# A fast matrix product in fp32 on one core: a scheduler's model of transfers, the first sums of the weights, and where a bias is added

## The chip, the core and the metric

The kernel runs on one core of a Trainium2 chip. The core has TensorE (PE, matmuls into PSUM), VectorE (DVE), ScalarE (ACT), GpSimd (POOL) and SyncE (SP, which here only issues DMAs). GpSimd also issues DMAs, among them accumulating ones, which add what they bring to what lies in the target. The metric is the device time in microseconds of one execution; the median of several runs counts.

## What is computed

```python
# x: 1024 x 512, weight: 64 x 512 x 512, lin_w: 512 x 512, lin_b: 512, all float32
out_lin = x @ lin_w.T + lin_b
xv = jnp.einsum('bf,efm->bem', x, weight)
zp = jnp.einsum('bf,efm->bem', jnp.square(x), jnp.square(weight))
interaction = 0.5 * jnp.sum(jnp.square(xv) - zp, axis=1)
return out_lin + interaction
```

The costly part is xv, 64 products of 1024 x 512 by 512 x 512, of which only the sum of squares over the 64 is kept.

## The kernel before

**Groups and trees.** The weights are cut into 16 groups (`NG`). A group holds four quadrants of 1 MB, w11, w12, w21 and w22 (w22 has two buffers, w22a and w22b). Each group's product is made by Strassen's scheme, in Winograd's form, twice over: seven outer products, and each of these again by seven inner ones. One outer product is a `tree(s, g, i)`, in the order `ORDER = (1, 6, 2, 7, 5, 4, 3)`. An inner product (`product`, L481) is two fp32 matmuls of 128x128 by 128x512; the profile shows each such matmul as two records. So a tree has 28 records and a group 196.

**Sums that the scheme needs.** On the side of x there are seven blocks X1 to X7, made once, at the start. Each block has its four parts (copies on ScalarE or sums of 1024 elements a row on VectorE) and inner sums of 256 (`x_sum`), four a block, in seven slots. On the side of the weights, tree 5 takes T1 = w11 + w12 and tree 6 takes T2 = w11 + w12 + w22. `outer_sum` makes these by DMA: it loads w11 into T1 or T2 once more and adds the other quadrants by accumulating DMAs (`load_more`, L422) issued by GpSimd. Later w12 += w22 (before tree 7) and w21 += T2 (before tree 4) are made in the same way. The inner sums `t` of each tree's weights are GpSimd adds of 512.

**From PSUM to the output.** There are four pairs of PSUM banks: b1, b3, b2_0 and b2_1. Within a tree, product 5 goes to b3 and is copied out, product 3 is added there and copied again; product 1 goes to b1 and is copied to a b2 pair, to which products 6, 7 and 4 add. Between these, VectorE takes the sums out (`whole`), and GpSimd finishes some of them. Product 7 can only start when VectorE has taken the b2 pair after product 6 (`outer_sbuf(b2, p53, 1)`). Finished parts are squared on ScalarE and summed over the 64 on VectorE (L297) into acc. For zp the weights are squared on ScalarE (`w_squares`) and summed on VectorE into w2_sum.

**Start.** x and lin_w come in eight and four chunks of 256 KB on SP's and ScalarE's queues, the bias on GpSimd's. Three matmuls of zeros (L326) run first. Then 64 records of x @ lin_w.T (L340) fill all four bank pairs; the last four of them stand behind product 5 of the first tree. VectorE adds the bias on the way out of PSUM (eight adds of 512), and the result, lin, goes to DRAM.

**End.** lin and the sums of 15 groups come back from DRAM (lin into the freed w21 and T1, the sums into T2 and w22a), x comes back and is squared with a factor of -0.5, VectorE adds up (L607), TensorE makes zp's part (L627, 64 records), and VectorE's last adds go to the output.

**The order is planned.** No engine's order is written by hand. `Plan.add` takes each operation with what it costs on an engine, what it reads and writes, and for a DMA how long after its issue it lands (`land`). `Plan.order` first gives each operation a latest time, from TensorE's fixed order (`key`) back through the dependencies; then it plays the kernel forward and lets each engine take the ready operation that is due first. The order found is the order in which instructions are issued; each engine works in that order and waits by semaphores. So a wrong cost in the plan costs no time itself, but it places instructions. SP's DMAs cost 2.4 or 4.8 us of SP's time in the plan, and land 1.5 later; accumulating ones land 8 later. Several DMAs under way don't slow each other in it. `both=True` marks VectorE operations that are planned longer when GpSimd works beside them.

Of the kernel before, what the change touches and what calls it, by code (L numbers as in the profile page):

```python
# [11 lines left out]
F32 = mybir.dt.float32  # L12
# [4 lines left out]
P = 128  # L17
# [9 lines left out]
class Plan:  # L27
# [6 lines left out]


    HOP = 0.3

    def __init__(self):
        self.ops = []
        self.writer = {}  # L40
        self.readers = defaultdict(list)

    def add(self, costs, emit, reads=(), writes=(), key=None, land=0.0, both=False):
        op = SimpleNamespace(
            n=len(self.ops), costs=costs, emit=emit, key=key, land=land,
            deps=set(), succ=[], latest=None, end=None, both=both,
        )
        for r in reads:
            if r in self.writer:
                op.deps.add(self.writer[r])  # L50
        for w in writes:
            op.deps.update(self.readers[w])
            if w in self.writer:
                op.deps.add(self.writer[w])
        for r in reads:
            self.readers[r].append(op.n)
        for w in writes:
            self.writer[w], self.readers[w] = op.n, []
        op.deps.discard(op.n)
        self.ops.append(op)  # L60

    def order(self):
# [11 lines left out]
        while stack:  # L74
            o = stack.pop()
            latest = t if o.latest is None else o.latest
            cost = min(o.costs.values()) + o.land + self.HOP
            for x in o.succ:
                latest = min(latest, ops[x].latest - cost)
            o.latest = latest  # L80
            for d in o.deps:
                waiting[d] -= 1
                if not waiting[d]:
                    stack.append(ops[d])
# [3 lines left out]
        free = dict.fromkeys(pending, 0.0)  # L88
        running = dict.fromkeys(pending)
        times = [self.HOP]  # L90
        done, late, nxt = [], 0.0, 0

        def release(o):
            for e in o.costs:
# [16 lines left out]
        def pick(e, now):  # L111
            if e == PE:
                if nxt < len(chain):
                    o = chain[nxt]
                    if not left[o.n] and ready(o) <= now + 1e-6:
                        return o
                return None
            at = {n: ready(ops[n]) for n in pending[e]}
            for n in sorted((n for n in at if at[n] <= now + 1e-6),
                            key=lambda n: (ops[n].latest, n)):  # L120
                o = ops[n]
                until = now + o.costs[e]
                if not any(
                    now + 1e-6 < at[u] < until - 0.2
                    and ops[u].latest < o.latest
                    and ops[u].latest + late < until + 0.1
                    for u in at
                ):
                    return o
            return None  # L130

        while len(done) < len(ops):
            now = heapq.heappop(times)
            moved = True
            while moved:
                moved = False
                for e in pending:
                    if free[e] > now + 1e-6:
                        continue
                    o = pick(e, now)  # L140
                    if o is None:
                        continue
                    moved = True
                    if e == PE:
                        nxt += 1
                        late = max(late, now - o.latest)
                    cost = o.costs[e]

                    if e == DVE and o.both and free[POOL] > now + 0.1:
                        over = free[POOL] - now  # L150
                        cost += 0.9 * over
                        longer(POOL, 0.35 * over)
                    elif e == POOL and free[DVE] > now + 0.1 and running[DVE].both:
                        over = free[DVE] - now
                        cost += 0.5 * over
                        longer(DVE, 0.9 * over)
                    free[e] = now + cost
                    running[e] = o
                    o.end = free[e] + o.land
                    heapq.heappush(times, free[e])  # L160
                    heapq.heappush(times, o.end + self.HOP)
                    for f in o.costs:
                        pending[f].discard(o.n)
                    done.append((o, e))
                    for x in o.succ:
                        left[x] -= 1
                        if not left[x]:
                            release(ops[x])
# [4 lines left out]
def kernel(  # L173
# [70 lines left out]
        return take  # L244

    half = [P, 2, N]
    for i in range(1, 8):
        make(f"X{i}", [P, 7, Q])
    for q in ("w11", "w12", "w21", "w22a", "w22b", "T1", "T2"):
        make(q, [P, 2, 2, N])  # L250
    for pos in range(4):
# [7 lines left out]
    b2_ring = ring("b2", 2, [P, G, N], ps)  # L259
    acc_ring = ring("acc", 2, [P, NB, MG])  # L260
    w2_sum = sb.tile([P, NK, M], F32, tag="w2_sum", name="w2_sum")
    bias = buf["t4_1"]
    acc_dram = dram.tile([P, NB, M], F32, tag="accd", name="accd")
    lin_dram = dram.tile([P, NB, M], F32, tag="lind", name="lind")

# [34 lines left out]
            reads, writes,  # L300
        )

    def dma(o, i, reads, writes, cost=2.4, land=1.5, queue=nc.sync):
        plan.add({SP: cost}, lambda _: queue.dma_start(o, i), reads, writes, land=land)


    x_src = xT.rearrange("(p k) b -> p k b", k=NK)
# [4 lines left out]
    for k in range(NK):  # L312
        q, r = divmod(k, KH)
        x0, x1, l = f"oa{q}", f"oa{2 + q}", f"ob{q}"
        nc.sync.dma_start(buf[x0][:, r, :], x_src[:, k, ts(0, H)])
        nc.scalar.dma_start(buf[l][:, r, :], lw_src[:, k, :])  # L316
        nc.sync.dma_start(buf[x1][:, r, :], x_src[:, k, ts(1, H)])
        for name in (x0, l, x1):
            landing((name, r), 4.0 + 2.5 * k)
    nc.gpsimd.dma_start(bias, lin_b.partition_broadcast(P))  # L320


    zero = buf["t1_0"]
    nc.vector.memset(zero, 0.0)
    for j in range(3):
        nc.tensor.matmul(  # L326
            buf[("b1", "b3")[j // 2]][:, j % 2, :], zero[:, 0:P], zero, start=True, stop=True
        )
    plan.add({PE: 4.0}, None, (), ("b1", "b3"), key=-2000)

    lin_banks = ["b3", "b1", "b2_0", "b2_1"]
    for k in range(NK):
# [16 lines left out]
                     (bank,), key=PLACE[5] + 0.5 if late else -1000 + 4 * k + g)  # L349
    for g, bank in enumerate(lin_banks):  # L350
        o = ("ob2", "ob3", "c_0", "c_1")[g]
        for j in range(G):
            costs, emit = two_input(DVE, buf[o][:, j, :], buf[bank][:, j, :], bias, False, 512)
            plan.add(costs, emit, (bank, "t4_1"), ((o, j),))
        dma(lin_dram[:, ts(g, G), :], buf[o], ((o, 0), (o, 1)), (o,))

    def block4(i):
        return buf[f"X{i}"][:, 0:4, :].rearrange("p (k q) b -> p k (q b)", k=2)
# [11 lines left out]
    for i, n in ((1, "A11"), (2, "A12"), (4, "A22")):  # L370
        act(block4(i), a_ap(n), None, a_parts(n), (f"X{i}",))

    def x_sum(i, o, a, b, kind, reads, size):

        if kind != "-a - b":
            costs, emit = two_input(DVE, o, a, b, kind == "a - b", size)
        else:
            costs = two_input(DVE, o, a, b, True, size)[0]

            def emit(_):  # L380
                nc.vector.scalar_tensor_tensor(o, a, -1.0, b, ALU.mult, ALU.subtract)

        plan.add(costs, emit, reads, (f"X{i}",), both=True)

    for i, a, b, kind in (
        (5, "A22", "A21", "a - b"),
        (6, "X5", "A11", "-a - b"),
        (7, "A11", "A21", "a - b"),
        (3, "X6", "A12", "-a - b"),
    ):  # L390
        x_sum(i, block4(i), a_ap(a), a_ap(b), kind, a_parts(a, b), 1024)
    for i in ORDER:
        x = buf[f"X{i}"]
        a11, a21, a12, a22 = (x[:, s, :] for s in range(4))
        s1, s2, s4 = (x[:, s, :] for s in range(4, 7))
        for o, a, b, kind in (
            (s1, a21, a22, "a + b"),
            (s2, s1, a11, "a - b"),
            (s4, a12, s2, "a - b"),
            (a21, a11, a21, "a - b"),  # L400
        ):
            x_sum(i, o, a, b, kind, (f"X{i}",), 256)
    for n in a_buf.values():
        plan.add({SP: 0.0}, None, (), (n,) + tuple((n, r) for r in range(KH)))
    for n in ("ob0", "ob1", "ob2", "ob3", "c_0", "c_1"):
        plan.add({SP: 0.0}, None, (), (n, (n, 0), (n, 1)))


# [4 lines left out]

    def load(g, q):
        n = w(g, QUAD[q])
        dma(buf[n], weight[g, q], (), (n,), 4.8)

    def load_more(n, src, reads=()):

        plan.add(  # L420
            {POOL: 1.0},
            lambda _: nc.gpsimd.dma_start(buf[n], src, accum_op=ALU.add),  # L422
            (n,) + reads, (n,), land=8.0,
        )

    def outer_sum(g, which):
        if which < 3:
            n = f"T{which}"
            dma(buf[n], weight[g, 0], (), (n,), 4.8)
            for q in (1, 3)[:which]:  # L430
                load_more(n, weight[g, q])
        elif which == 3:
# [119 lines left out]

    for g in range(NG):
        acc_name[g] = acc_ring()
        load(g, 0)
        outer_sum(g, 2)
        for q in (1, 2, 3):
            load(g, q)
        outer_sum(g, 1)
        w_squares(g, "w12")  # L560
        for idx, i in enumerate(ORDER):
            if i == 1:
# [26 lines left out]
    for g in range(NB // G):  # L589
        n, a = lin_all[g], acc_all[g]  # L590
        dma(buf[a][:, :, 0:edge], acc_dram[:, ts(g, G), 0:edge],
            tuple(("accd", x) for x in range(NG - 1)), (a,))
        dma(buf[n], lin_dram[:, ts(g, G), :], (), (n,))
    for n in xe.values():
        plan.add(
            {DVE: 1.24},
# [80 lines left out]
```

## Time and profile before

| what | value |
|---|---|
| median of three runs | 1419.26 us (1419.24 to 1420.74) |
| the profiled execution's own time | 1420.72 us |
| its span, first to last instruction | 1418.9 us |
| mean granted TensorE clock in the span | 0.999 |
| mean DMA rate | 142 GB/s |
| T<-weight on SP (32, 1 MB each), issue to landing | 4.8 us |
| T<-weight on GpSimd (48, accumulating, 1 MB each) | 8.2 us |
| w<-T on GpSimd (16, accumulating, 1 MB each) | 6.9 us |
| T<-lind and w<-lind on SP (2 each, 512 KB each) | 4.3 and 4.4 us |
| t<-lin_b on GpSimd (the bias, 256 KB) | 6.5 us |

The page counts an instruction's time from its start to its end; matmuls are pipelined, so a matmul's length overlaps the next one's, and the pace is read from start to start. A timeline's row is a run of like instructions on one engine: its start in the span, its length, the engine, the line, what it writes and reads, how many; in brackets, how long the engine had been idle before it and what released it. A row of VectorE at L276 is an add or a subtraction whichever helper made it, so rows are told apart by their tiles.

### The profile page before, as it was taken

The numbers are of one execution on the slowest core, as the hardware profiler recorded it, in microseconds if no ns is written. First come the engines' busy times: TensorE is split into PE (matmuls) and PEld (weight loads), VectorE is DVE, ScalarE is ACT, GpSimd is POOL, SyncE is SP. The second block draws the span as 40 slices with busy tenths as digits, with TensorE's granted clock in tenths as the row PEclk, the third lists the DMA queues.
The fourth block names the chain that finished last, engine by engine and source line by source line (L and its number), as shares of the span: only waits on it lengthen the run. The fifth ranks groups of instructions, "written<-read, shape, count | busy, mean of one in ns | idle before, by whom it ended". The sixth has DMA issues, their size and how long they took to land.

```text
span 1418.9 us, 10383 instructions
## 1 busy us (share of the span) xinstructions
PE 1408.6 (99%) x3270; PEld 621.9 (44%) x3270; DVE 1082.0 (76%) x957; ACT 681.8 (48%) x692; POOL 1014.1 (71%) x693
## 2 busy tenths in 40 slices
PE   9999999999999999999999999999999999999998
PEld 4444444444444444444444444444444444444443
DVE  4779596876958678596877959687795867869685
ACT  2346363554635446373544636355463644537331
POOL 3587786867769686786958678586777868678660
PEclk9999999999999999999999999999999999999999
DMA  9666372655737275472746637265573727546331
GB/s 327 184 162 167 95 179 74 189 123 148 176 88 162 86 182 148 118 178 73 182 108 168 162 100 182 74 182 122 148 181 90 162 79 191 139 123 144 102 106 60
DMA packets 47286, 200.96 MB, mean 142 GB/s; under 512 B 19008, under 2 KB 20032, under 8 KB 24704
## 3 DMA queue, kind: packets, MB, share of 16 engines
q0 software_dynamic: 11600, 84.15, 31.4%
q1 hardware_dynamic: 35056, 115.09, 22.7%
q10 hardware_dynamic: 576, 1.05, 0.2%
q8 instruction: 27, 0.44, 0.1%
q14 instruction: 27, 0.22, 0.0%
HBM read 177.34 MB, written 6.16 MB: 129 GB/s over the span
## 4 chain that ended last, share of the span: by engine, by line
PE 95%; DMA 2%; DVE 2%; POOL 1%; issue 0%; ACT 0%; ACTq 0%; DVEq 0%; SPq 0%
PE b L481 93%; PE b L627 2%; DMA w<-weight 1%; DVE X L276 1%; DMA ob<-lin_wT 1%; POOL ob L276 0%; POOL c L276 0%; DVE w_sum L297 0%; DVE c L276 0%; DVE ob L276 0%; POOL oa L276 0%; ACT oa L290 0%; ACTq L316 0%; POOL t L276 0%; DVE p L276 0%
## 5 line engine op out<-in xcount | busy, mean ns | idle before, releaser
L481 PE MATMUL b<-t,X 128*128 128x512 f32 x1792 | 808.2, 593 | 4.0 <-DVE oa L276 2.6
L481 PEld LDWEIGHTS b<-t,X 128*128 128x128 f32 x1792 | 340.4, 190 | 434.8 <-issue 429.0
L481 PE MATMUL b<-w,X 128*128 128x512 f32 x768 | 358.1, 592 | 0.0
L276 POOL TENSOR_TENSOR t<-w 128x512 f32<-128x512 f32 x128 | 171.2, 1337 | 147.6 <-PE b L481 91.8
L288 ACT COPY p<-b 128x1024 f32<-128x1024 f32 x160 | 161.1, 1007 | 170.6 <-PE b L481 170.6
L481 PEld LDWEIGHTS b<-w,X 128*128 128x128 f32 x768 | 145.9, 190 | 183.7 <-issue 183.4
L276 POOL TENSOR_TENSOR t<-w,t 128x512 f32<-128x512 f32 x128 | 167.7, 1310 | 57.7 <-PE b L481 57.7
L290 ACT ACTIVATE oa<-oa 128x1024 f32<-128x1024 f32 x128 | 133.7, 1057 | 148.0 <-DVE oa L276 146.1
L297 DVE TENSOR_REDUCE acc<-oa 128x16 f32<-128x1024 f32 x128 | 153.7, 1212 | 39.2 <-ACT oa L290 39.2
L481 PE MATMUL b<-T,X 128*128 128x512 f32 x384 | 180.5, 592 | 0.0
L288 ACT COPY b<-b 128x1024 f32<-128x1024 f32 x112 | 111.8, 999 | 141.0 <-PE b L481 140.5
L297 DVE TENSOR_REDUCE w_sum<-wsq 128x16 f32<-128x1024 f32 x128 | 152.2, 1209 | 9.2 <-ACT wsq L290 9.2
L290 ACT ACTIVATE c<-c 128x1024 f32<-128x1024 f32 x64 | 67.6, 1057 | 160.2 <-DVE c L276 93.7
L276 DVE TENSOR_TENSOR oa<-b,p 128x1024 f32<-128x1024 f32 x96 | 116.9, 1218 | 34.5 <-PE b L481 34.5
L276 POOL TENSOR_TENSOR t<-T 128x512 f32<-128x512 f32 x64 | 85.3, 1333 | 65.7 <-issue 35.4
L481 PEld LDWEIGHTS b<-T,X 128*128 128x128 f32 x384 | 73.1, 190 | 92.4 <-issue 84.9
L276 DVE TENSOR_TENSOR p<-b,p 128x1024 f32<-128x1024 f32 x80 | 97.7, 1221 | 20.8 <-PE b L481 19.1
L276 DVE TENSOR_TENSOR ob<-b,p 128x1024 f32<-128x1024 f32 x48 | 58.6, 1221 | 70.2 <-PE b L481 70.2
L290 ACT ACTIVATE wsq<-w 128x1024 f32<-128x1024 f32 x96 | 98.2, 1057 | 15.1 <-DMA w<-weight 13.3
L276 POOL TENSOR_TENSOR t<-T,t 128x512 f32<-128x512 f32 x64 | 86.4, 1350 | 18.1 <-PE b L481 18.1
L276 DVE TENSOR_TENSOR p<-b,oa 128x1024 f32<-128x1024 f32 x32 | 39.2, 1224 | 65.6 <-PE b L481 65.6
L276 DVE TENSOR_TENSOR oa<-b,oa 128x1024 f32<-128x1024 f32 x64 | 78.3, 1223 | 9.8 <-PE b L481 9.7
(55 smaller groups left out, 1338.7 us busy)
## 6 DMA issues: line engine op xcount, KB each, us to landing
w<-weight SPq DMA_DIRECT2D x48, 1024.0 KB, 4.9
T<-weight POOLq DMA_DIRECT2D x48, 1024.0 KB, 8.2
T<-weight SPq DMA_DIRECT2D x32, 1024.0 KB, 4.8
w<-weight POOLq DMA_DIRECT2D x16, 1024.0 KB, 8.2
w<-T POOLq DMA_DIRECT2D x16, 1024.0 KB, 6.9
w22a<-weight SPq DMA_DIRECT2D x8, 1024.0 KB, 11.1
w22b<-weight SPq DMA_DIRECT2D x8, 1024.0 KB, 11.3
oa<-xT SPq DMA_DIRECT2D x8, 256.0 KB, 6.4
```

The lines of the kernel that those rows point to most:

```text
L276: f(o, a, b)
L288: nc.scalar.copy(o, i)
L290: nc.scalar.activation(o, i, func)
L297: lambda _: nc.vector.tensor_reduce(o, i.rearrange("p a (m e) -> p a m e", e=E), axis=AX.X, op=ALU.add),
L481: nc.tensor.matmul(buf[b][:, j, :], buf[f"X{i}"][:, SLOT[p], ts(j, P)], op, start=first, stop=True, skip_group_check=True,)
L627: nc.tensor.matmul(buf[bank][:, j, :], buf[xe[h, k // KH]][:, k % KH, ts((g * G + j) % (NB // 2), P)], w2_sum[:, k, :], start=(k == 0), st ...
```

## The change

The diff has five parts.

1. The plan's model of transfers. A DMA now costs SP 0.45 us, GpSimd 0.9, and has a time on the wire (`move`) which all DMAs share, one after the other (`wire`), and then lands. SP may issue a DMA only when it is due within 50 us (`AHEAD`). The landings of the first chunks are set a little later.
2. T1 and T2 of group 0 are made by VectorE from the loaded quadrants, two adds of 1024 each, and not by DMA. The loads of each group stand ahead of its sums in the program.
3. The inner sums of x are made for X1 alone (four operations of 256) and then for X2 to X7 together (four of 1536), in one tile that holds all seven.
4. lin leaves PSUM by four ScalarE copies of 1024 and goes to DRAM without the bias. At the end each of the four target buffers is filled with the bias by two broadcast DMAs on SP, and lin is added by an accumulating DMA.
5. Two matmuls of zeros run at the start instead of three.

```diff
+    AHEAD = 50.0
...
-            cost = min(o.costs.values()) + o.land + self.HOP
+            cost = min(o.costs.values()) + o.move + o.land + self.HOP
...
+                if e == SP and o.latest - self.AHEAD > now + 1e-6:
+                    heapq.heappush(times, o.latest - self.AHEAD)
+                    return None
...
+                    if o.move:
+                        wire = max(wire, free[e]) + o.move
+                        o.end = wire + o.land
...
+    x_all = sb.tile([P, 7, 7, Q], F32, tag="x_all", name="x_all")
     for i in range(1, 8):
-        make(f"X{i}", [P, 7, Q])
+        buf[f"X{i}"] = x_all[:, i - 1]
...
-    def dma(o, i, reads, writes, cost=2.4, land=1.5, queue=nc.sync):
-        plan.add({SP: cost}, lambda _: queue.dma_start(o, i), reads, writes, land=land)
+    def dma(o, i, reads, writes, move=1.75):
+        plan.add({SP: 0.45}, lambda _: nc.sync.dma_start(o, i), reads, writes, land=2.0, move=move)
...
-            landing((name, r), 4.0 + 2.5 * k)
-    nc.gpsimd.dma_start(bias, lin_b.partition_broadcast(P))
+            landing((name, r), 4.3 + 2.6 * k)
...
-    for j in range(3):
+    for j in range(2):
         nc.tensor.matmul(
-            buf[("b1", "b3")[j // 2]][:, j % 2, :], zero[:, 0:P], zero, start=True, stop=True
+            buf["b1"][:, j, :], zero[:, 0:P], zero, start=True, stop=True
         )
...
         o = ("ob2", "ob3", "c_0", "c_1")[g]
-        for j in range(G):
-            costs, emit = two_input(DVE, buf[o][:, j, :], buf[bank][:, j, :], bias, False, 512)
-            plan.add(costs, emit, (bank, "t4_1"), ((o, j),))
-        dma(lin_dram[:, ts(g, G), :], buf[o], ((o, 0), (o, 1)), (o,))
+        act(buf[o], buf[bank], None, (bank,), (o,))
+        dma(lin_dram[:, ts(g, G), :], buf[o], (o,), (("lind", g),))
...
-    for i in ORDER:
-        x = buf[f"X{i}"]
-        a11, a21, a12, a22 = (x[:, s, :] for s in range(4))
-        s1, s2, s4 = (x[:, s, :] for s in range(4, 7))
+    for lo, hi in ((0, 1), (1, 7)):
+        a11, a21, a12, a22, s1, s2, s4 = (x_all[:, lo:hi, s, :] for s in range(7))
+        names = tuple(f"X{i + 1}" for i in range(lo, hi))
         for o, a, b, kind in (
             (s1, a21, a22, "a + b"),
             (s2, s1, a11, "a - b"),
             (s4, a12, s2, "a - b"),
             (a21, a11, a21, "a - b"),
         ):
-            x_sum(i, o, a, b, kind, (f"X{i}",), 256)
+            x_sum(names, o, a, b, kind, names, Q * (hi - lo))
...
-        dma(buf[n], weight[g, q], (), (n,), 4.8)
+        dma(buf[n], weight[g, q], (), (n,), 3.5)
...
-            {POOL: 1.0},
+            {POOL: 0.9},
             lambda _: nc.gpsimd.dma_start(buf[n], src, accum_op=ALU.add),
-            (n,) + reads, (n,), land=8.0,
+            (n,) + reads, (n,), land=2.5, move=5.5,
         )
 
     def outer_sum(g, which):
-        if which < 3:
+        if g == 0 and which < 3:
+            o, a, b = (("T1", "w11", "w12"), ("T2", "w22a", "T1"))[which - 1]
+            for c in range(NCB):
+                costs, emit = two_input(DVE, buf[o][:, c], buf[a][:, c], buf[b][:, c], False)
+                plan.add(costs, emit, (a, b), (o,), both=True)
+        elif which < 3:
             n = f"T{which}"
-            dma(buf[n], weight[g, 0], (), (n,), 4.8)
+            dma(buf[n], weight[g, 0], (), (n,), 3.5)
...
-        load(g, 0)
-        outer_sum(g, 2)
-        for q in (1, 2, 3):
+        for q in range(4):
             load(g, q)
         outer_sum(g, 1)
+        outer_sum(g, 2)
...
-        dma(buf[n], lin_dram[:, ts(g, G), :], (), (n,))
+        for j in range(G):
+            dma(buf[n][:, j, :], lin_b.partition_broadcast(P), (), (n,), 1.0)
+        load_more(n, lin_dram[:, ts(g, G), :], (("lind", g),))
```

## The prediction

> **What bounds the kernel now.** I read the page's busy row first, then TensorE's timeline from end to end, then the timeline of the engine that ends each of its gaps.
>
> ```profile
> PE 1408.6 (99%) x3270; PEld 621.9 (44%) x3270; DVE 1082.0 (76%) x957; ACT 681.8 (48%) x692; POOL 1014.1 (71%) x693
> ...
> PEclk9999999999999999999999999999999999999999
> DMA  9666372655737275472746637265573727546331
> ```
>
> TensorE has work almost all the time and no other engine is near full, so only time at which TensorE doesn't advance can be won. Its pace without a wait is read from any long row, such as 66.60 to 71.75 for 12 records: 0.429 us a record, and two records make one fp32 matmul. 3270 records at 0.429 are 1403 us of a span of 1418.9. The other 16 us are start, gaps and end; the timeline of TensorE shows all of them.
>
> ```profile
> 1.46 4.64 PE L326 MATMUL b<-t 128*128 128x512 f32 x6 [1.46 <-DVE t L324]
> 5.93 25.91 PE L340 MATMUL b<-ob,oa 128*128 128x512 f32 x60
> 33.01 1.96 PE L481 MATMUL b<-t,X 128*128 128x512 f32 x4 [1.16 <-DVE ob L276]
> 34.80 1.88 PE L340 MATMUL b<-ob,oa 128*128 128x512 f32 x4
> ...
> 45.10 1.88 PE L481 MATMUL b<-T,X 128*128 128x512 f32 x4
> 49.35 3.68 PE L481 MATMUL b<-t,X 128*128 128x512 f32 x4 [2.37 <-DVE oa L276]
> 52.83 1.91 PE L481 MATMUL b<-T,X 128*128 128x512 f32 x4
> ...
> 1371.27 1.88 PE L481 MATMUL b<-w22b,X 128*128 128x512 f32 x4
> 1373.15 1.95 PE L481 MATMUL b<-t,X 128*128 128x512 f32 x4
> 1375.32 1.98 PE L481 MATMUL b<-w22b,X 128*128 128x512 f32 x4 [0.22 <-DVE oa L276]
> 1377.58 1.98 PE L481 MATMUL b<-t,X 128*128 128x512 f32 x4 [0.27 <-DVE oa L276]
> 1379.71 1.96 PE L481 MATMUL b<-t,X 128*128 128x512 f32 x4
> ```
>
> Columns: start, length, then the work. Four records should take 1.72 us from start to start. **Gap A**: 60 records from 5.93 should hand over at 31.68; the next start is 33.01, and its four take 1.79, so 1.40 is lost. **Gap B**: four from 45.10 should hand over at 46.82, the next start is 49.35 (2.53 lost), and the four after it take 3.48, half speed, with the next four 0.03 late: 1.79 more. Together 4.32. **Gap C**: the steps at the end are 1.88, 2.17, 2.26, 2.13 and 1.80 instead of 1.72: 1.66 lost. Between 55 and 1371 no start is late. The zero matmuls at the start take 4.47 us (1.46 to 5.93).
>
> Who is late in A and B is VectorE:
>
> ```profile
> 18.04 1.42 DVE L276 TENSOR_TENSOR X<-X 128x256 f32<-128x256 f32 x4
> 28.65 1.22 DVE L297 TENSOR_REDUCE w_sum<-wsq 128x16 f32<-128x1024 f32 x1 [9.19 <-ACT wsq L290]
> ...
> 31.58 1.28 DVE L276 TENSOR_TENSOR ob<-b,t 128x512 f32<-128x512 f32 x2
> ...
> 39.29 8.87 DVE L276 TENSOR_TENSOR X<-X 128x256 f32<-128x256 f32 x8
> 48.08 1.21 DVE L276 TENSOR_TENSOR oa<-b,p 128x1024 f32<-128x1024 f32 x1
> ```
>
> VectorE stands idle 9.19 us with X sums ready, because next in its written order is a reduction whose square waits for w12 until 27.57. So the bias adds that empty b3 start at 31.58, though its last matmul ended near 5.93 + 52 x 0.429 + 0.2 = 28.4 (A), and eight X sums run from 39.29 at 1.10 us each, not 0.34, because GpSimd adds run beside them; the add that product 7 needs waits behind them (B). The order was written with four loads due earlier than they came.
>
> **Part by part, against the profiled execution (1420.72 us).**
>
> Third zero matmul removed. In the timeline of weight loads, each beside the record before its own, the zeros' stand at 1.46 (two), 2.48, 3.33, 4.18 and 5.04 and lin's first at 5.51; so records two to six start at 2.48 to 5.51, and lin at 5.93. With four zero records lin takes the fifth's place, 5.04, if its data is there. Its two chunks land about 4.7: SP's fifth issue, at 4.67, was released by the first lin_w chunk, and the first x chunk was no later. **Gain 0.90, bounds 0.5 and 0.9.** A rule speaks against it: the Trainium skill (TensorE: Matmul & The Clock Gate, "Why this matters for your kernels") wants 4 us of matmuls to warm the clock, and 4 x 0.85 are 3.4. In this trace the pace turns from 0.85 to 0.43 between 5.04 and 5.51, 3.6 to 4.0 us after the first. By the rule, lin begins cold, which costs nothing against zeros: cold lin still advances, cold zeros don't. A cold stretch longer by one 3.4 us window (the page, "What's actually happening") would cost 3.4/2 = 1.7 and make this part -0.8. The row stands nearer, as lin follows without a hole: I keep 0.9.
>
> Bias leaves the start. Out: 8 VectorE adds (1.28 per pair, 5.1 us) and the 256 KB broadcast on POOL's queue. In: 4 ScalarE copies from PSUM, about 1.0 each by the row of the p copies (1.01). ScalarE was busy 10.3 us of 32 to 54, so four more fit. b3 has its 52nd record's end near 5.04 + 52 x 0.429 + 0.2 = 27.5 after the shift, the copy is done by 29 if ScalarE isn't held, and the first product wants b3 at 5.04 + 60 x 0.429 = 30.8. What can hold it is a square queued ahead that waits for a load. **A: gain 1.2 of 1.40**, bounds 0 and 1.4.
>
> Wide sums of x. Before, 28 sums of 256, 16.4 us busy. After, 4 of 256 and 4 of 1536. From paces, start to start, 256 take 0.335 and 1024 take 1.14, so 1536 take about 1.68 (estimate from these two rows): 1.3 + 6.7 = 8.0. They can't start until all seven X blocks are there: the last x chunk lands near 12.9 (ScalarE's wait for it ends 12.27, VectorE's last block from x is at 13.96), and three blocks of 1.14 after it end near 16.5, so the wide sums end near 23 with nothing in between.
>
> T1 and T2 of group 0. Out: 2 loads and 3 accumulating DMAs of 1 MB, and 3 POOL triggers of 0.86. In: 4 VectorE adds of 1024, 1.14 each: 4.6 us. Inputs: T2's load had landed by 15.64 and w11 by 18.00, about 2.4 us per MB with nothing beside them; so in order w11, w12, w22a, w21 land near 15.6, 18, 20.4 and 22.8. Before, w12 took until 27.5. VectorE from 13: 3.4 of blocks, 6.7 wide, 4.6 for T, 2.3 of w12's reductions: T2 is ready near 30. Beside POOL's four t adds of w11 (18.00 to 24.4 before) the two engines hold each other up; the worst row, 1.10 for 0.34, adds at most POOL's own 6.4 us. So between 27.7 (reductions later) and 36.4. Product 5 of the second tree, the first user, is due at 37.65 (30.8 + 4 products x 1.72), and POOL needs one t add of 1.3 to 1.9 before it. Met in the middle by over 5 us, short by 0.6 at the worst end.
>
> With these VectorE has no X sums left after 39, and the add before product 7 starts when its bank is ready. **B: gain 4.2 of 4.32**; bounds 0 (another late operation takes the place) and 4.32. The half-speed stretch goes with the gap: after an idle of 2.37 four records took 3.48, after the 1.16 of A 1.79, and the granted clock of 32 to 54 is 0.92. The same page and section put the fall after about 3.4 us of idling; by that B's 2.5 would stay warm and its removal would be worth 2.5 only. The row decides: 4.3.
>
> The model of transfers only writes another order; no instruction gets longer. What it moves: SP no longer issues more than 50 us ahead of a due time. w22b went out at 36.32 for a first use at 193.63; that moves to a stretch where the DMA share is 0.55. T2's chain (load at 82.79, first product straight from T2 at 133.55) is held only until 133.6 - 25 (its three links by the planner's new costs) - 50 = 59, before its buffer is free. The waits at 55 to 1371 cost TensorE nothing now, so nothing is to be won there: **0**, bounds 0 and a loss of 3 (15 groups at 0.2).
>
> Bias at the end. Out: 4 loads of 512 KB on SP. In: 8 bias broadcasts of 256 KB on SP (issue 0.35 to 0.45 each) and 4 accumulating DMAs on POOL (0.86 each), each waiting for its two broadcasts. Behind a waiting trigger on POOL stand the t adds of the last tree (1371.79, 1373.02) and the oa add at 1374.26. Bounds: a 1 MB accumulate took 8.2 us, so 512 KB less; the broadcast at the start took 6.5 in full traffic, the 256 KB stores at the end 2.2. The w21 pair, free at 1371.6, would be complete near 1371.6 + 2 + 4 + 7 = 1385 instead of 1376. Its adds on VectorE ran at 1377.45 and 1385.18; moved later they leave VectorE to the trees in gap C, and they are not needed before 1398.27, when the first output add ran. POOL's 3.4 us of triggers and their waits work the other way. **C: gain 0.4**, bounds +1.6 and -4. The end from 1390 is 56 records of TensorE and one output add; nothing of it changes.
>
> Sum: 0.9 + 1.2 + 4.2 + 0 + 0.4 = 6.7. From the profiled 1420.72 that is 1414.0. The three runs were 1419.24, 1419.26 and 1420.74, so the profiled one stands at their upper end; from the median it would be 1412.6. The half-speed stretch of B, 1.8 us, may be what sets it apart, and then 1414.0 counts. I reckon from the middle of the two, 1420.0: **1413.3**.
>
> **Rivals.**
> 1. The head keeps a gap (12%): T2, or the square in front of a bank copy, is late, TensorE waits 2 to 3 us near 37 and the clock halves again for 3.4 us. For it: the tight worst end above. Against: w12 comes some 9 us earlier. A loss of 4.3 leaves 6.7 - 4.3 = 2.4: 1417.6.
> 2. Slower by POOL's waiting triggers at the end (10%): four accumulations each hold POOL until a broadcast has landed. If it stands 3 us at each of four, 12 us, the last trees' t adds come late; TensorE loses about 10 and a half-speed stretch of 1.8: 6.3 - 11.8 is 5.5 slower, 1425.5. It decides from about 9 us of standing. For it: an in-order queue and waits that weren't there. Against: T1's pair comes 12 us before w21's, and the planner counts 3.5 us for a broadcast.
> 3. No new order without a price (6%): one wait of 0.4 us in each of 15 groups eats 6: 1419.3. Against: no late start in 1300 us now.
>
> **Numbers.** The forecast's case has 72%, with its own range 1410.8 to 1416.4. Apart by over 0.2% (2.8 us, about what a measurement can tell here): faster below 1416.4, slower above 1422.1. Of rival 1 a third is still faster (a shorter wait) and the rest between, as is rival 3; of rival 2 a fifth ends between. Faster 0.76, same 0.16, slower 0.08. The range goes from all gaps closed (1419.26 - 0.9 - 1.4 - 4.3 - 1.7 = 1411.0, rounded down) to rival 1's 1417.6.
>
> **What would show it.** Lin starts at 5.0; the first product at 30.8 with no gap from VectorE; four records at 1.72 throughout 30 to 60 and a clock that stays full; T2's adds done by 36; w12's squares begin before 21, not 27.6; VectorE's X sums 8 instead of 28, all before 30; no late start in the groups. Wrong would be a gap near 37 ended by POOL's t, one ended by ScalarE's copy of a lin bank, or, near 1360 to 1385, POOL idle on a DMA.

## The result and the profile after

| | before | after |
|---|---|---|
| median (runs) | 1420.0 us (8; 1418.01 to 1421.02) | 1414.91 us (8; 1414.23 to 1415.85) |
| ratio, 95% interval | | 0.9965, 0.9954 to 0.9976 |
| profiled span | 1418.9 us | 1413.5 us |
| start of the last matmul record | 1413.69 us | 1408.08 us |

The change is 0.35% faster, 5.1 us of medians, and 5.61 us at TensorE's last record. The page's busy row and its chain by engine, of the changed kernel:

```profile
PE 1405.5 (99%) x3268; PEld 621.4 (44%) x3268; DVE 1079.4 (76%) x933; ACT 680.6 (48%) x696; POOL 1012.5 (72%) x693
...
PE 99%; DVE 1%; issue 0%; DVEq 0%
```

No engine's busy time moved by more than 3.1 us, and TensorE still sets the end: between its first matmul and its last the chain holds one stretch of another engine. So the gain must lie in TensorE's gaps and in its pace. Its timeline (start, length, work, then in brackets what ended an idle stretch):

```profile
1.46 3.78 PE L333 MATMUL b<-t 128*128 128x512 f32 x4 [1.46 <-DVE t L331]
5.04 26.64 PE L347 MATMUL b<-ob,oa 128*128 128x512 f32 x60
31.52 1.88 PE L490 MATMUL b<-t,x_all 128*128 128x512 f32 x4
33.23 1.88 PE L347 MATMUL b<-ob,oa 128*128 128x512 f32 x4
...
45.25 1.88 PE L490 MATMUL b<-t,x_all 128*128 128x512 f32 x4
46.97 1.88 PE L490 MATMUL b<-T,x_all 128*128 128x512 f32 x4
...
1334.46 1.88 PE L490 MATMUL b<-t,x_all 128*128 128x512 f32 x4
1338.05 3.67 PE L490 MATMUL b<-t,x_all 128*128 128x512 f32 x8 [1.71 <-DVE oa L284]
...
1369.03 1.88 PE L490 MATMUL b<-t,x_all 128*128 128x512 f32 x4
1370.74 1.88 PE L490 MATMUL b<-w22b,x_all 128*128 128x512 f32 x4
1372.46 3.60 PE L490 MATMUL b<-t,x_all 128*128 128x512 f32 x8
```

Gaps A (31.7) and B (47) are gone: from 31.52 on, each four records take 1.72. Gap C after 1360 is gone too: the steps from 1369.03 are 1.71 and 1.72. But the 60 lin records take 26.48 from 5.04 to 31.52, not 25.75, since the clock is still at half speed for the first of them. And there is a **new gap D**: four records from 1334.46 should hand over at 1336.18, and the next starts at 1338.05.

**Accounts.** The trace's record of the granted clock gives the time at which it rises: 5.11 before, 6.50 after. Until then a record takes 0.85 us, after it 0.43, so a rise that comes 1 us later costs 0.5. With that, the start of the last record in every profile of this study is

last record = 1401.17 + 0.86 x (zero matmuls) + rise / 2 + what TensorE lost by waiting.

Here 0.86 is a zero matmul's two records at the full clock. The constant was set by one run (the bias at the start, below). A second run without any late start (squares on ScalarE, below), with its rise 1.8 us earlier, gives the same constant within 0.01. For the pair: A 1.40, B 4.32, C 1.66 and one zero 0.86 come in; the later rise takes 0.70 and D 1.95. Sum 5.59 of 5.61.

ScalarE's squares of w12 and then VectorE after, in the timelines of the start:

```profile
17.42 2.00 ACT L298 ACTIVATE wsq<-w 128x1024 f32<-128x1024 f32 x2 [4.03 <-DMA w<-weight]
```

```profile
17.49 1.73 DVE L284 TENSOR_TENSOR T<-w,w 128x1024 f32<-128x1024 f32 x1 [1.71 <-DMA w<-weight]
19.14 2.82 DVE L284 TENSOR_TENSOR x_all<-x_all 128x1536 f32<-128x1536 f32 x1
21.89 2.28 DVE L284 TENSOR_TENSOR T<-w,w 128x1024 f32<-128x1024 f32 x1
24.09 1.75 DVE L284 TENSOR_TENSOR x_all<-x_all 128x1536 f32<-128x1536 f32 x1
...
28.56 1.21 DVE L284 TENSOR_TENSOR T<-w22a,T 128x1024 f32<-128x1024 f32 x1
29.70 1.75 DVE L284 TENSOR_TENSOR x_all<-x_all 128x1536 f32<-128x1536 f32 x1
31.37 2.33 DVE L305 TENSOR_REDUCE w_sum<-wsq 128x16 f32<-128x1024 f32 x2
```

The 9.19 us of idling before is gone: w12 is there at 17.4, ten microseconds earlier. T2 is done at 29.8 and the last sum of x at 31.4, where before X sums ran until 51. The question is which of the five parts did this.

### The profile page after: what moved, and what is told of

It is laid out like the page before. It is cut to its first block, busy times and chain, and to the rows that moved or that the text cites. A ratio compares the mean times of both kernels' runs of the same rounds, so it can differ in the third digit from the quotient of the medians.

```text
span 1413.5 us, 10316 instructions
## 1 busy us (share of the span) xinstructions
PE 1405.5 (99%) x3268; PEld 621.4 (44%) x3268; DVE 1079.4 (76%) x933; ACT 680.6 (48%) x696; POOL 1012.5 (72%) x693
## 4 chain that ended last, share of the span: by engine, by line
PE 99%; DVE 1%; issue 0%; DVEq 0%
PE b L490 95%; PE b L347 2%; PE b L637 2%; DVE w L607 0%; PE b L333 0%; DVE oa L284 0%; DVE acc L305 0%; DVE w22a L284 0%; DVEq L683 0%; DVE t L331 0%
## 5 line engine op out<-in xcount | busy, mean ns | idle before, releaser
L490 PE MATMUL b<-t,x_all 128*128 128x512 f32 x1792 | 806.1, 592 | 1.7 <-DVE oa L284 1.7
L490 PEld LDWEIGHTS b<-t,x_all 128*128 128x128 f32 x1792 | 340.3, 190 | 430.7 <-issue 423.6
L490 PE MATMUL b<-w,x_all 128*128 128x512 f32 x768 | 358.1, 592 | 0.0
L490 PEld LDWEIGHTS b<-w,x_all 128*128 128x128 f32 x768 | 145.9, 190 | 183.7 <-issue 172.7
L284 POOL TENSOR_TENSOR t<-w,t 128x512 f32<-128x512 f32 x128 | 174.1, 1360 | 66.7 <-PE b L490 66.5
L490 PE MATMUL b<-T,x_all 128*128 128x512 f32 x384 | 180.4, 592 | 0.0
L284 POOL TENSOR_TENSOR t<-T 128x512 f32<-128x512 f32 x64 | 91.7, 1433 | 58.1 <-issue 33.1
L490 PEld LDWEIGHTS b<-T,x_all 128*128 128x128 f32 x384 | 73.0, 190 | 91.8 <-issue 91.8
L284 POOL TENSOR_TENSOR c<-oa,p 128x1024 f32<-128x1024 f32 x32 | 89.3, 2791 | 0.1
L284 POOL TENSOR_TENSOR ob<-ob,p 128x1024 f32<-128x1024 f32 x32 | 89.3, 2789 | 0.0
```

The source lines that it names most:

```text
L284: f(o, a, b)
L490: nc.tensor.matmul(buf[b][:, j, :], buf[f"X{i}"][:, SLOT[p], ts(j, P)], op, start=first, stop=True, skip_group_check=True,)
```

## The experiments

Each run's loss by waiting comes from the formula above, and its place from the timeline. "New" and "old" are the planner's transfer model; part 2 is T1 and T2 on VectorE, 3 the wide sums, 4 the bias at the end. The expectations set theories against each other. For gaps A and B: M blames the order planned with too early landings, T the transfers at the start, V VectorE's own work, and W the work and the traffic together. For gap D, D1 blames a square beside GpSimd's operations. For the zeros, Z1 ties the clock's rise to TensorE's first work, Z2 does not.

| run | model, parts, zeros | median us | rise | lost by waiting, us |
|---|---|---|---|---|
| before | old, none, 3 | 1420.0 | 5.11 | A 1.40, B 4.32, C 1.66 |
| after | new, 2 3 4, 2 | 1414.91 | 6.50 | D 1.95 |
| model alone | new, none, 3 | 1433.84 | 6.86 | 16.3 near 39, 3.2 in C |
| without the model | old, 2 3 4, 2 | 1413.45 | 6.85 | 0.88 after 1370 |
| squares marked | new, 2 3 4, 2 | 1413.55 | 6.98 | D 0.81 |
| three zeros | new, 2 3 4, 3 | 1415.13 | 4.43 | D 1.94 |
| T alone | old, 2, 3 | 1415.81 | 6.12 | A 0.27, C 1.68 |
| T by DMA | new, 3 4, 2 | 1430.85 | 6.82 | 17.6 near 38 |
| narrow sums | new, 2 4, 2 | 1415.09 | 6.12 | D 1.94 |
| bias at the start | new, 2 3, 2 | 1413.64 | 7.03 | none |
| squares on ScalarE | new, 2 3 4, 2 | 1412.95 | 5.24 | none |
| one zero | new, 2 3, 1 | 1414.79 | 7.87 | 0.74 for data near 4 |
| bias at the start, old model | old, 2 3, 2 | 1420.54 | 5.82 | A 5.9, C 1.7 |

### The transfer model alone

The kernel before with part 1:

```diff
+                if e == SP and o.latest - self.AHEAD > now + 1e-6:
...
+                    if o.move:
+                        wire = max(wire, free[e]) + o.move
...
-        dma(buf[n], weight[g, q], (), (n,), 4.8)
+        dma(buf[n], weight[g, q], (), (n,), 3.5)
```

> The kernel before with part 1 of the change alone: the planner's new transfer model (wire, SP's issue 50 us ahead at most, later landings). Every instruction stays, only orders move. Theory M (the order was planned with loads due too early, and that alone opened gaps A and B): VectorE no longer stands idle about 9 us behind the square of w12, gaps A (1.4 us) and B (4.3 us) close, span near 1413 to 1414. Theory W (the gaps close because work and traffic leave the start: bias adds, T1 and T2 by DMA, small sums of x): at least half of A and B stays, span 1416 or more, first products after 33 us or a half-speed stretch between 35 and 60 us.

Ratio 1.0089 (1.0074 to 1.0104): slower by 13 us. Theory M falls. GpSimd's timeline in this run:

```profile
30.22 0.88 POOL L430 DMA_DIRECT2D w<-weight  x1 [2.98 <-ACT wsq L298]
30.81 1.18 POOL L430 DMA_DIRECT2D T<-weight  x1
34.52 1.27 POOL L284 TENSOR_TENSOR t<-w 128x512 f32<-128x512 f32 x1 [2.54 <-PE b L489]
35.75 0.84 POOL L430 DMA_DIRECT2D T<-weight  x1
51.86 1.25 POOL L284 TENSOR_TENSOR t<-T 128x512 f32<-128x512 f32 x1 [15.26 <-DMA T<-weight]
```

T2's second addition is the third trigger, behind w12's and T1's and behind a t add that waits for TensorE; in the kernel before it was the first of the three, at 28.21. It goes out at 35.75 and lands 16 us later beside the other accumulations, while TensorE stands 13.6 us and then runs at half speed. Under the new model the planner put this chain last; which item of part 1 does that (the shared wire, the new costs or the limit on SP) no run separates. Gap A, meanwhile, is gone in this run: VectorE's bias adds for b3 start at 30.14, not behind an X sum.

### T1 and T2 by VectorE alone

The kernel before with part 2, old planner:

```diff
+        if g == 0 and which < 3:
+            o, a, b = (("T1", "w11", "w12"), ("T2", "w22a", "T1"))[which - 1]
+            for c in range(NCB):
+                costs, emit = two_input(DVE, buf[o][:, c], buf[a][:, c], buf[b][:, c], False)
+                plan.add(costs, emit, (a, b), (o,), both=True)
...
```

> The kernel before with part 2 alone: T1 and T2 of group 0 are four VectorE adds, loads in front of sums. Old transfer model, old small sums, bias at the start, three zeros. Theory T (the start's transfers made the gaps: five of nine MB leave, so w12 lands near 18 us instead of 27.5 and nothing holds VectorE): gaps A and B both close, first product near 31.7, no late start from then to 60 us; span 1412.5 to 1414. Theory V (VectorE's own work made them, 16.4 us of small sums and 5.1 of bias adds, to which 4.6 come): A or B stays with 1.4 us or more, span 1415 or more.

Theory T holds: ratio 0.9972 (0.9961 to 0.9983), A shrinks to 0.27, B is gone. TensorE's timeline:

```profile
6.44 25.91 PE L340 MATMUL b<-ob,oa 128*128 128x512 f32 x60
32.38 1.95 PE L486 MATMUL b<-t,X 128*128 128x512 f32 x4
34.17 1.88 PE L340 MATMUL b<-ob,oa 128*128 128x512 f32 x4
...
46.19 1.88 PE L486 MATMUL b<-t,X 128*128 128x512 f32 x4
```

Here VectorE still has 28 small sums and eight bias adds, and small sums run as late as 49. Six of them run ahead of the bias adds for b3, from 28.95 to 30.96, and A's 0.27 is likely theirs; no other start before 60 us is late. VectorE still idles once, 5.93 us, but only until w12 lands at 18.1 (its square runs at 18.06), so its work after that is in time. The span, 1414.1, lies 0.1 above what was expected: the clock rose late (6.12) and C stays, at 1.68.

### The changed kernel without part 2

```diff
-        if g == 0 and which < 3:
+        if False:
```

> The changed kernel with part 2 taken back: T1 and T2 of group 0 by loads and accumulating DMAs, all else as changed. Theory T: TensorE waits for T2 near 38 us as in the run with the transfer model alone, 10 us or more, span 1423 or more. Theory V: with small sums and bias adds gone VectorE is free, gap under 2 us before 60 us, span under 1416.

Ratio 1.0084 (1.0067 to 1.0100). By its timeline TensorE waits 15.35 us for a t add on T2, then runs at half speed:

```profile
35.11 3.60 PE L490 MATMUL b<-w,x_all 128*128 128x512 f32 x8
54.05 5.65 PE L490 MATMUL b<-t,x_all 128*128 128x512 f32 x8 [15.35 <-POOL t L284]
```

So part 2 is not only enough for most of the gain; without it the rest of the change loses 10 us. The edit leaves the group's loads ahead of its sums in the program, and still w12's squares begin only at 27.40: that order in the program alone does not bring w12 sooner.

### The changed kernel without the model, and without model and part 4

The first run puts back the old costs and landings and takes out the wire and the limit on SP:

```diff
-    AHEAD = 50.0
...
-        plan.add({SP: 0.45}, lambda _: nc.sync.dma_start(o, i), reads, writes, land=2.0, move=move)
+        plan.add({SP: cost}, lambda _: queue.dma_start(o, i), reads, writes, land=land)
```

> The changed kernel with the old transfer model put back, parts 2 to 5 kept. Theory M: VectorE or ScalarE again waits for a load in front of ready work, a gap of 2 us or more before 60 us, span 1415.5 or more. Theory W: no gap before 60 us, as w12 lands near 17.5 us without the T traffic in front of it; span within 1 us of 1413.5, apart from what the end does.

No gap before 60 us, as theory W has it, and T. It has 0.88 of late starts after 1370 and no D, and its runs (1413.29 to 1414.09) lie below all of the changed kernel's. Beside these parts the model wins nothing. The second run takes part 4 back too, so that VectorE adds the bias at the start:

> The changed kernel with the bias back at the start and the old transfer model: parts 2, 3 and 5 alone. Theory T (part 2 closes the gaps, the model is not needed for it): no late start before 60 us beyond 0.3. The model's worth is then only what the end shows: if the new model places the end better, the late starts of the kernel before come back after 1360, 1.2 to 1.7 us in sum, span 1413 to 1414.5; if not, 1412.2 as with the new model.

(Its edit is the one above together with that of the next section.) The forecast for the start failed. All of the gain is gone (ratio 1.0002, 0.9993 to 1.0011), by a gap A of 4 us with a half-speed stretch behind it; C is back as well. TensorE's timeline:

```profile
5.04 26.31 PE L341 MATMUL b<-ob,oa 128*128 128x512 f32 x60
35.31 2.54 PE L486 MATMUL b<-t,x_all 128*128 128x512 f32 x4 [3.96 <-DVE ob L276]
37.63 3.04 PE L341 MATMUL b<-ob,oa 128*128 128x512 f32 x4
```

In the changed kernel, ScalarE's timeline has the copy of the first lin bank as soon as it is full:

```profile
28.28 1.01 ACT L296 COPY ob<-b 128x1024 f32<-128x1024 f32 x1 [8.86 <-PE b L347]
```

In the run without model and part 4 the same work stands on VectorE, behind T2 and a wide sum; its timeline:

```profile
31.08 1.21 DVE L276 TENSOR_TENSOR T<-w22a,T 128x1024 f32<-128x1024 f32 x1
32.22 1.74 DVE L276 TENSOR_TENSOR x_all<-x_all 128x1536 f32<-128x1536 f32 x1
33.89 2.47 DVE L276 TENSOR_TENSOR ob<-b,t 128x512 f32<-128x512 f32 x4
```

The bank is full near 28, as there, and is emptied from 33.89. With small sums (T alone) the same planner let the bias adds in at 30.96.

### The changed kernel with the bias at the start, and with narrow sums

```diff
-        act(buf[o], buf[bank], None, (bank,), (o,))
+        for j in range(G):
+            costs, emit = two_input(DVE, buf[o][:, j, :], buf[bank][:, j, :], bias, False, 512)
+            plan.add(costs, emit, (bank, "t4_1"), ((o, j),))
...
```

> The changed kernel with part 4 taken back: eight bias adds on VectorE at the start, the bias broadcast on GpSimd's queue, plain loads of lin at the end. Theory T: no gap before 60 us, as w12 still lands early. Theory V: gap A of 1 us or more at 31.5. At the end both expect what the old end gave or less: late starts of 0.2 to 0.5 us each after 1360, 1.7 in sum at most; the gap of 1.95 us at 1336 stays if it comes from a square beside GpSimd's adds, and goes if the bias DMAs or their waits made it.

No late start anywhere, D included, and its runs (1413.23 to 1414.06) lie below all of the changed kernel's. By its expectation, D's going would speak for the bias DMAs; the section on gap D shows why it does not. The new planner, asked for the same VectorE adds, puts the first two between T2's first half and a wide sum (VectorE's timeline):

```profile
26.88 1.21 DVE L284 TENSOR_TENSOR T<-w22a,T 128x1024 f32<-128x1024 f32 x1
28.55 1.29 DVE L284 TENSOR_TENSOR ob<-b,t 128x512 f32<-128x512 f32 x2 [0.46 <-PE b L349]
29.75 1.75 DVE L284 TENSOR_TENSOR x_all<-x_all 128x1536 f32<-128x1536 f32 x1
```

So the model does have a worth beside parts 2 and 3: with the bias on VectorE it is 7.6 us (A 5.9 and C 1.7 against nothing). At the start, part 4 and the model each cover for the other, and the change has both. The sums of x were undone by one line:

```diff
-    for lo, hi in ((0, 1), (1, 7)):
+    for lo, hi in ((0, 1), (5, 6), (1, 2), (6, 7), (4, 5), (3, 4), (2, 3)):
```

> The changed kernel with part 3 taken back in its work: 28 sums of 256 instead of 4 and 4 of 1536. Theory T: VectorE's sums take more time, but nobody waits: no gap before 60 us, span within 0.8 of 1413.5 (the clock's rise at the start moves it by that much). Theory V: a gap of 1 us or more in front of product 7 of the first tree, near 45 us.

As theory T has it: the loss is D's 1.94, the same as with wide sums (1.95). With the new planner and ScalarE's copies, part 3 is worth nothing.

### Gap D: the square behind GpSimd

The changed kernel's timelines of GpSimd and of VectorE at the gap:

```profile
1330.06 0.88 POOL L426 DMA_DIRECT2D w<-T  x1 [0.94 <-PE b L490]
1330.66 2.66 POOL L284 TENSOR_TENSOR oa<-p,oa 128x1024 f32<-128x1024 f32 x1
1332.99 1.56 POOL L284 TENSOR_TENSOR t<-T 128x512 f32<-128x512 f32 x1
1336.48 1.27 POOL L284 TENSOR_TENSOR t<-w22b 128x512 f32<-128x512 f32 x1 [1.93 <-issue]
```

```profile
1330.66 4.99 DVE L607 SCALAR_TENSOR_TENSOR w<-w 128x1024 f32<-128x1024 f32 x1
1335.57 1.21 DVE L305 TENSOR_REDUCE acc<-oa 128x16 f32<-128x1024 f32 x1
1336.70 1.21 DVE L284 TENSOR_TENSOR oa<-b,p 128x1024 f32<-128x1024 f32 x1
```

A square (1.26 us at 1322.07 in the same kernel) starts with GpSimd's add and ends 1.1 us after the second of GpSimd's two operations (1334.55), so it seems to have stood through both. Behind it stand a reduction and then the sum that product 7 waits for. Two runs tried it. The first only tells the planner that GpSimd holds the squares up:

```diff
-            (n,), (n,),
+            (n,), (n,), both=True,
```

> The changed kernel; the four squares of x at the end are marked as operations that GpSimd's adds hold up, so that the planner keeps them apart. Theory D1 (the new gap of 1.95 us at 1336 is a square of 1.26 us that ran 4.99 us beside two GpSimd operations, with the sum for product 7 queued behind it): no square over 2.5 us, no gap at 1336, span 1411.3 to 1411.8. Theory D2 (the gap comes from another cause, such as the DMAs that GpSimd issues there): the sum for product 7 is late again, span 1413 or more.

Neither expectation was met: the square is placed as before and takes 4.98, but the reduction behind it moved, so D falls to 0.81. The second takes the squares off VectorE:

```diff
-            {DVE: 1.24},
-            lambda _, x=buf[n]: nc.vector.scalar_tensor_tensor(
-                x, x, -0.5, x, ALU.mult, ALU.mult
-            ),
+            {ACT: 1.07},
+            lambda _, x=buf[n]: nc.scalar.activation(x, x, AF.Square, scale=0.5 ** 0.5),
...
```

(The last add, not shown here, then subtracts where it added.)

> The changed kernel with the four squares of x at the end on ScalarE (square of x times the root of one half) and subtracted in the last add instead of added; nothing of the result is left out. Theory D1 (a square of VectorE that starts beside a run of GpSimd operations waits until GpSimd pauses, and the gap at 1336 is that wait): the sums behind it run on time, no late start at 1336, the last matmul 1.9 us earlier for the same rise of the clock, span 1411.2 to 1412.4. Theory D2 (another operation or the DMAs there make it): a late start of 1 us or more between 1325 and 1345.

D is gone, as D1 says, with the bias DMAs still in place, and TensorE doesn't start late once after its first product. The span, 1410.9, lies below the 1411.2 to 1412.4 that were expected, as the clock rose early (5.24). TensorE's timeline at the place:

```profile
1332.12 1.88 PE L490 MATMUL b<-w,x_all 128*128 128x512 f32 x4
1333.84 5.31 PE L490 MATMUL b<-t,x_all 128*128 128x512 f32 x12
1338.98 1.88 PE L490 MATMUL b<-w,x_all 128*128 128x512 f32 x4
```

It is the best version: median 1412.95 (1412.34 to 1413.71), ratio to before 0.9948 (0.9933 to 0.9964). The interval overlaps that of the change, but its four runs all lie below the changed kernel's eight. In the run with the bias at the start, the same square begins a hundredth before GpSimd's t add, and there it is GpSimd that waits (VectorE's timeline, then GpSimd's):

```profile
1328.10 1.21 DVE L609 SCALAR_TENSOR_TENSOR w<-w 128x1024 f32<-128x1024 f32 x1
```

```profile
1328.11 2.34 POOL L284 TENSOR_TENSOR t<-T,t 128x512 f32<-128x512 f32 x1 [0.38 <-PE b L494]
```

The square takes its own 1.21, the t add 2.34 for 1.27. So D went there because the order is another, and not because the bias DMAs did. What decides which engine goes on is not shown: in the changed kernel, too, the square's start is marked first, by 0.004 us, and there it was the square that waited.

### The zero matmuls

```diff
-    for j in range(2):
+    for j in range(3):
...
```

> The changed kernel with the third matmul of zeros put back, in b1. Theory Z1 (the clock rises a fixed time after TensorE's first work, and two zero matmuls are too few to cover it): lin starts at 5.93, the clock rises near 5.1 as in the kernel before, the first product starts at 31.7 against 31.5, 0.2 us slower. Theory Z2 (the rise falls at a time that doesn't depend on the number of zeros and differs from run to run by up to 1.7 us or so): the rise lies anywhere from 5 to 8 us, and the third zero costs 0.43 to 0.9 us for a given rise.

The second run has one, on top of the bias at the start:

```diff
-    for j in range(2):
+    for j in range(1):
```

> The changed kernel with the bias back at the start (no late start after the first product in its run) and one matmul of zeros instead of two. Theory Z2 (the clock's rise keeps its own time; a zero matmul costs 0.86 us at full pace where data could have run): lin starts at about 4.75, when its first chunks land, against 5.04; the rise anywhere from 4.4 to 8.5; 0 to 0.3 us faster than with two for the same rise. Theory Z1 (the rise needs unbroken work from the start, so the pause from 3.3 to 4.75 puts it off): the rise at 8.2 us or later, 0.5 us or more slower.

With three, the clock rose at 4.43, the earliest of all and before the 5 to 8 that Z2 gave, which by the formula won back the third zero's 0.86 in that execution. Over the profiles, the rise lies at 4.43, 5.11, 6.12 and 6.86 with three zeros and at 5.24, 5.82, 6.12, 6.50, 6.82, 6.85, 6.98 and 7.03 with two, so Z1's fixed time falls. The trace agrees with the Trainium skill (TensorE: Matmul & The Clock Gate, "What's actually happening"), which has the clock judged in free-running windows of 3413 ns: in the kernel before the stretches between two changes of the clock are 44.37 and 3.41 us, 13 windows and one. Where a window boundary falls is chance, so one profile can't price a zero matmul. With one zero, TensorE stands from 3.5 to 4.65 until data lands, as its timeline has it:

```profile
1.46 2.07 PE L335 MATMUL b<-t 128*128 128x512 f32 x2 [1.46 <-DVE t L333]
4.65 27.60 PE L349 MATMUL b<-ob,oa 128*128 128x512 f32 x60 [1.11 <-DMA ob<-lin_wT]
```

It loses 0.74 by that and wins 0.86, next to nothing for the same rise; but the rise came at 7.87, and its five runs (1414.23 to 1415.81) lie above the four with two zeros (1413.23 to 1414.06). In the profiled execution the pause did put the rise off. A window of this run ended at 4.45 (7.87 less 3.41), nearly where the run with three zeros had its rise (4.43); there the clock rose, here only a window later, 1.7 us of work. Counted from the starts of its records, TensorE had stood 1.7 us in that window here and 0.6 there. How often this happens, and whether three zeros bring the rise forward on average, stays open, with one trace of each.

## The prediction against the runs

**The total** was right: 1413.3 with 1410.8 to 1417.6, against 1414.91; 6.7 us were forecast from the middle of the runs, 5.1 came. That it came so near is in part luck: C won 1.26 more than forecast, for a reason that stays open, and D, which was not foreseen, took 1.95.

**A and B** were right in size: 1.2 and 4.2 forecast, 1.40 and 4.32 came, the half-speed stretch of B with them. The steps of the transfers' part held: w11, w12 and w22a in time, w12's squares at 17.42 (before 21 was asked), T2 ready at 29.8 (27.7 to 36.4), a sum of 1536 at a pace of 1.67 (1.68). Two signs came late: the first product at 31.52 (30.8), as the clock rose late, and the end of the last X sum at 31.4 (before 30), for which no matmul waited.

**Whose gain it is** was in part wrong. The forecast gave A to the bias adds that leave VectorE and B to T1, T2 and the wide sums together, because no X sums would be left after 39. The runs show the traffic: taking two loads and three accumulations of group 0 away closes both gaps to 0.27 under the old planner, with the bias adds in place and small X sums until 49, while the new planner without this loses 13 us. The wide sums are worth nothing. Moving the bias adds off VectorE, given 1.2, is worth nothing at the start under the new planner and 5.9 us under the old one with wide sums; the parts are not terms of a sum.

**The third zero** was given 0.9, with bounds of 0.5 and 0.9. The place was right (lin at 5.04), and 0.86 is its price for a given rise. The step that failed is the bound: the clock rose 1.4 us later, which the rule's reading in the text allowed for (-0.8 for one more window) and the range of this term left out. It came to 0.16.

**C** was given 0.4, for bias adds that come later and leave VectorE to the trees. C went altogether, +1.66, and the runs don't give it to one part. Under the old planner it is 1.66, 1.68 and 1.7 with the old end, and 0.88 of late starts stay with the new one. Under the new planner it is 3.2 in the run with the model alone, and gone in all others, with either end. Why stays open.

**"The model of transfers only writes another order; no instruction gets longer"**, given 0, missed D, -1.95: another order put a square beside GpSimd's operations, and there it did get longer. The bound was a loss of 3 spread over the groups; it came in one place of the last group, where nothing had been looked for. D is not the model's alone: with that square on VectorE, every profile with the new model and parts 2 and 4 has it, and it is gone when any one of the three is taken back. Rival 1, a gap near 37 ended by GpSimd's t, came only where T2 is made by DMA under the new model (13.6 and 15.4 us). Rival 2, GpSimd's triggers waiting for the bias, didn't come: no trigger of these stands idle, though the broadcasts landed 6.4 and 5.6 us after issue, more than the 4 reckoned with.

So 6.7 becomes 5.6 in four steps: the zero brought 0.74 less, A and B 0.32 more, C 1.26 more, and D took 1.95.

## What to carry to other kernels

A list scheduler that is given a new model of one resource can move its worst chain elsewhere: change its model and the work together, and run each alone to know which one pays. Where an in-order engine idles with ready work behind a wait, look first for traffic that needn't be there at that moment, before the order. And when a stretch is nearly perfect, write its end as a constant plus known losses: here that told 0.1 us apart in single profiles, where the runs of one kernel lay 0.6 to 3.6 us apart.

## What the runs showed of the hardware

**VectorE and GpSimd held each other up** where an operation of VectorE with both inputs in SBUF met one of GpSimd. In gap D a square of 1.26 took 4.99, to 1.1 us behind two GpSimd operations; a sum of 1536 took 2.82 for 1.75; and in the other direction a GpSimd add of 1.27 took 2.34. The add at 1336.70, with one input in PSUM, took its 1.21 beside GpSimd's add of 1336.48. That agrees with the Trainium skill (GPSIMD Engine Reference, "Specifications"), which has GpSimd's SBUF interfaces shared with VectorE, with contention for VectorE's instructions with two SBUF inputs. How long the one that waits stands is not settled by these rows: in gap D through two operations, while in the kernel before X sums from 39.29 on and GpSimd's adds took turns.

**The clock is judged window by window.** TensorE's pause of 2.5 us in the kernel before cost a half-speed stretch of 3.41, 1.8 us of work; the pauses of 1.3 (A) and 1.9 (D) cost none. Windows of 3.413 us, counted on from each run's rise, and TensorE's idle time in each, summed from its records' starts at 0.43 us a record, fit all of these: a window with 2.53 (gap B), 2.41 (T by DMA) or 2.25 us of idling (bias at the start under the old model) was followed by half speed, one with 1.95 (the window before that 2.25) or 1.94 (D with three zeros) was not. So in these runs the limit lies between 1.95 and 2.25 us in one window, and where a window's end splits a pause, each part counts for itself. The Trainium skill (TensorE: Matmul & The Clock Gate, "Why this matters for your kernels") wants pauses under about 3 us; here 2.5 was too long, and the measurement decides.
